# Layer 3 of a graph network: transposes on row halves, reciprocals by DMA, W_out product over two units

## The chip, the cores and the metric

The kernel runs on one core of a Trainium2 chip. The core has a matrix engine (TensorE, written PE in the profile; its weight loads are a row of their own, PEld), a vector engine (VectorE, DVE), a scalar engine (ScalarE, ACT), a general engine (GpSimd, POOL) and a queue engine (SyncE, SP), which here only starts DMAs. Each engine works through its own list of instructions in order; semaphores tie them together. PE writes to PSUM[...] and DVE or ACT take the results from there to SBUF. The metric is the time of one execution in microseconds (us), as the median of three runs.

## The reference

The input x holds 32 graphs of 512 nodes with 64 features. One adjacency matrix adj (512 x 512, scaled, mostly zero) serves all. There are four layers, each of the form x = x + f(relu(layernorm(x))). Layer 0 is a graph convolution, layer 1 two rounds of it, layer 2 an attention layer with additive scores. Most of the time goes to layer 3:

```python
def gat_layer(x, graph, W, b):
    h = x @ W
    s = jnp.einsum('bnd,bmd->bnm', h, h) * graph
    s = jnp.where(s == 0.0, NEG_INF, s)
    a = jax.nn.softmax(s, axis=2)
    return jnp.einsum('bnm,bmd->bnd', a, h) + b
heads = jax.vmap(lambda W, b: gat_layer(flow_x, graph, W, b))(Wh, bh)   # 8 heads, 128 wide
x = jax.nn.leaky_relu(cat, negative_slope=0.01)     # cat: the heads side by side, 1024 wide
out = gat_layer(x, graph, W_out, b_out)             # 64 wide
return jax.nn.leaky_relu(out, negative_slope=0.01)
```

So each graph needs nine 512 x 512 softmaxes in layer 3 and one in layer 2. Everything is 32-bit floating point.

## The kernel before

Layers 0 and 1 run first, to about 260 us. Layers 2 and 3 are one pipeline over *units*, built by `run` near the end of the kernel. A unit is two softmaxes of 512 x 512, called k = 0 and 1, and there are 160 of them: 16 `Gat` units (layer 2, two graphs each), 128 `Heads` units (layer 3, one graph and two heads each, so four per graph) and 16 `Out` units (the last attention of layer 3, two graphs each). An Out unit stands after the third Heads unit of the graph that follows its two graphs, so in the steady part eight Heads units and one Out unit make up one repeat. The last Out unit stands alone, after three empty places.

A unit is worked in four steps, one for each block of 128 rows, r = 0 to 3. Step number k of the loop in `run` issues, in this order, the work of several units:

- `scores` (L545 to L550) of the current unit: one product for each of the two softmaxes, into `s_ps`, which has two buffers of two PSUM banks.
- `transpose` of the unit that began five steps ago. For block j of columns it turns the exponentials `p_att` around, eight blocks of 128 x 128 on PE, into two PSUM tiles `pt_ps` (L413), and ACT copies each tile to `pt_att` (L418).
- `recips` of the same unit, when j is 1. DVE takes the reciprocals of the row sums (L432). These lie one per partition; the later multiplication needs them along the free dimension, the same in all 64 partitions of a half. Eight products with a broadcast reciprocal as the weights and the identity as the moving matrix do this (L436), and ACT copies the result to `recb` (L444).
- `values` of the block transposed one step before: two products into `av` (L425), which is summed over four steps.
- `end` of the unit that began ten steps ago. `end(0)` multiplies `av` by `recb` on DVE (`o_att`, L448); for Heads `end(1)` makes two products `y_ps` (L619) and ACT turns them into the heads' outputs `cat` (L624); for Out `end(2)` transposes back and adds to x (L454, L456), and SP stores the result (L675).
- `prep` of the next unit. For Heads, step 2 makes `g` (L591, L599), and the first unit of a graph makes the normalised input `hn` and its transpose `hx` in step 0. For Out, the steps 0 to 3 multiply `cat` by `W_out`, two of the eight heads in each, into one PSUM tile `gT_ps` (L642); step 3 then copies it to `gT` and transposes that to `gV` (L648 to L653).
- `soft` of the current unit: DVE multiplies the scores by adj (L536), finds zeros (L540) and, for each k, adds the mask and takes the row minimum of the negated scores (L397); ACT takes the exponential and the row sum (L401).

Eight PSUM banks are in use: four for the scores, one for `av`, and three in the pool `ps_m`, from which the tiles `pt_ps`, `rec_ps`, `y_ps`, `g_ps`, `gT_ps`, `hx_ps`, `gV_ps` and `back_ps` are all taken. `recb` has two buffers.

The kernel is written with the Tile layer, which puts in the semaphores. It also places each engine's instructions when the program is built, so an instruction can stand earlier or later on its engine than the order of the calls says. No planner of the kernel's own is involved, and the SP and POOL queues have nothing in this part but the output stores.

## Time and profile before

| | us |
|---|---|
| median of three runs (lowest, highest) | 2912.98 (2911.55, 2920.7) |
| the profiled execution, its own time | 2918.14 |
| span of that execution, first to last instruction | 2916.4 |
| PE busy | 2813.4 (96%) |
| PE weight loads busy | 1380.0 (47%) |
| DVE busy | 2407.5 (83%) |
| ACT busy | 2049.0 (70%) |
| POOL busy | 52.7 (2%) |

The profile is of one execution. A group of instructions is named by the line of the kernel, the engine, the operation, and what it writes and reads; its duration is the mean of one instruction, and "idle before" is the time for which the engine stood still just before it, with the instruction that released it. Matmuls overlap, so the duration of one matmul is more than its share of the engine's time; the distance from one start to the next is what a matmul costs. In a timeline each row is a start, a length, the engine, and how many like instructions were merged into the row; in brackets stands the idle time before it and what ended it.

### The profile page before, as it was taken

Reading aid. Unit: us, or ns where it says so; the run is one execution under the profiler, and the core shown is the slowest. Engines: PE = TensorE matmul, PEld = TensorE weight load, DVE = VectorE, ACT = ScalarE, POOL = GpSimd, SP = SyncE. Lnnn points to the kernel's source line nnn. Section 1 sums busy time; section 2 is a strip of 40 time slices with the busy share of each in tenths; the row PEclk is TensorE's granted clock in tenths of the full one; section 3 lists DMA queues with packets and bytes.
Section 4 is the critical chain, followed back from the end, with each engine's and each line's share of the span. In section 5 each row is a group of like instructions: output and inputs, shape, how many; then the busy total and the mean of one; then the engine's idle time right before and its main releaser. Section 6 shows DMA issues by size and latency. Waiting matters only on the chain.

```text
span 2916.4 us, 41809 instructions
## 1 busy us (share of the span) xinstructions
PE 2813.4 (96%) x15532; PEld 1380.0 (47%) x15532; DVE 2407.5 (83%) x4870; ACT 2049.0 (70%) x4687; POOL 52.7 (2%) x49
## 2 busy tenths in 40 slices
PE   7998887899999999999999999999999999999998
PEld 4555544444444444444444444444444444444443
DVE  6665889899798988888888888888888888888884
ACT  2333767677777778777777777777777777777775
POOL 3000000000000000000000000000000000000000
PEclk9998999899999999999999999999999999999999
DMA  3000000000000000000000000000000000000000
GB/s 86 1 1 1 1 1 1 1 1 1 1 5 4 1 4 1 4 1 5 1 4 1 4 1 4 1 5 1 4 1 5 1 5 1 4 1 4 1 4 4
DMA packets 9916, 13.10 MB, mean 4 GB/s; under 512 B 1016, under 2 KB 9376, under 8 KB 9584
## 3 DMA queue, kind: packets, MB, share of 16 engines
q1 hardware_dynamic: 4752, 5.24, 0.5%
q10 hardware_dynamic: 4208, 4.19, 0.5%
q8 instruction: 122, 2.00, 0.3%
q0 software_dynamic: 752, 0.99, 0.2%
q14 instruction: 82, 0.67, 0.1%
HBM read 6.23 MB, written 4.19 MB: 4 GB/s over the span
## 4 chain that ended last, share of the span: by engine, by line
PE 88%; DVE 6%; ACT 3%; issue 1%; POOL 1%; DMA 1%; POOLq 0%; DVEq 0%; ACTq 0%
PE av L425 20%; PE pt_ps L413 20%; PE s_ps L547 19%; PE rec_ps L436 6%; PE g_ps L591 5%; PE y_ps L619 4%; PE nt_ps L240 4%; PE gT_ps L642 3%; PE nt1b_ps L240 2%; ACT p_att L401 1%; DVE s_att L536 1%; PE po L251 1%; DVE t_att L397 1%; PE wh_ps L474 1%; DVE l_att L397 1%
## 5 line engine op out<-in xcount | busy, mean ns | idle before, releaser
L401 ACT ACTIVATE p_att<-t_att,negmax 128x512 f32<-128x512 f32 x1152 | 825.3, 717 | 466.3 <-DVE negmax L397 466.2
L536 DVE TENSOR_TENSOR s_att<-s_ps,adj_p 128x1024 f32<-128x1024 f32 x576 | 703.3, 1221 | 228.6 <-PE s_ps L547 228.6
L413 PEld LDWEIGHTS pt_ps<-ident,p_att 128*128 128x128 f32 x5120 | 554.8, 142 | 492.6 <-ACT p_att L401 187.5
L418 ACT COPY pt_att<-pt_ps 128x512 f32<-128x512 f32 x1280 | 679.3, 581 | 120.7 <-PE pt_ps L413 120.5
L397 DVE CUSTOM_DVE_ANT_0 t_att<-s_att,t_att 128x512 f32<-128x512 f32 x1152 | 752.3, 687 | 13.4
L413 PE MATMUL pt_ps<-ident,p_att 128*128 128x128 f32 x5120 | 714.5, 282 | 12.6 <-ACT p_att L401 7.5
L547 PE MATMUL s_ps<-hx,g 64*128 64x512 f32 x2048 | 661.2, 625 | 2.0 <-DVE s_att L536 2.0
L425 PE MATMUL av<-pt_att,hn 128*64 128x512 f32 x2048 | 579.0, 611 | 0.0
L540 DVE TENSOR_SCALAR t_att<-s_att 128x1024 f32<-128x1024 f32 x576 | 393.1, 683 | 24.3 <-ACT pt_att L418 0.5
L547 PEld LDWEIGHTS s_ps<-hx,g 64*128 64x128 f32 x2048 | 204.8, 185 | 311.3 <-issue 121.3
L401 ACT ACTIVATION_READ_ACCUMULATOR p_att<-t_att,negmax 128x1 f32 x1152 | 216.0, 187 | 0.0
L436 PE MATMUL rec_ps<-ident,rec 128*64 128x128 f32 x2560 | 186.6, 284 | 16.9 <-DVE rec L432 10.6
L436 PEld LDWEIGHTS rec_ps<-ident,rec 128*64 128x64 f32 x2560 | 144.4, 139 | 50.6 <-issue 26.5
L624 ACT ACTIVATE cat<-y_ps,bh 128x512 f32<-128x512 f32 x256 | 159.6, 672 | 4.4 <-PE y_ps L619 4.4
L425 PEld LDWEIGHTS av<-pt_att,hn 128*64 128x64 f32 x2048 | 115.6, 135 | 76.5 <-issue 76.2
L619 PE MATMUL y_ps<-o_att,wh_sb 64*128 64x512 f32 x512 | 145.8, 641 | 1.6 <-ACT pt_att L418 0.8
L591 PE MATMUL g_ps<-hx,m 64*128 64x512 f32 x256 | 144.6, 645 | 1.0 <-ACT pt_att L418 0.9
L642 PE MATMUL gT_ps<-cat,wo_sb 128*64 128x512 f32 x512 | 131.4, 595 | 0.0
L448 DVE TENSOR_TENSOR o_att<-av,recb 128x512 f32<-128x512 f32 x160 | 108.9, 681 | 21.8 <-PE av L425 20.6
L240 PE MATMUL nt_ps<-adj_t,hn 128*128 128x512 f32 x256 | 116.5, 598 | 0.0
L397 DVE DVE_READ_ACCUMULATOR2_ANT negmax<- 128x1 f32 x1280 | 104.7, 82 | 0.0
L444 ACT COPY recb<-rec_ps 128x512 f32<-128x512 f32 x160 | 93.9, 587 | 8.8 <-PE rec_ps L436 8.8
(131 smaller groups left out, 1930.4 us busy)
## 6 DMA issues: line engine op xcount, KB each, us to landing
out_dram<-x SPq DMA_DIRECT2D x32, 128.0 KB, 1.8
x<-in_x_dram ACTq DMA_DIRECT2D x3, 1024.0 KB, 13.7
x<-in_x_dram ACTq DMA_DIRECT2D x4, 256.0 KB, 7.9
adj_raw<-in_adj_dram SPq DMA_DIRECT2D x1, 1024.0 KB, 5.3
wh_sb<-in_L_gnn_Wh_dram POOLq DMA_DIRECT2D x2, 256.0 KB, 8.0
wo_sb<-in_L_gnn_W_out_dram POOLq DMA_DIRECT2D x1, 256.0 KB, 7.9
wl<-in_L_gnn_net_params_dram POOLq DMA_DIRECT2D x4, 16.0 KB, 7.0
bias_b<-in_L_gnn_bias_dram POOLq DMA_DIRECT2D x1, 32.0 KB, 7.6
```

The lines of the kernel that those rows point to most:

```text
L240: nc.tensor.matmul(p, lhsT=lhs(k), rhs=adj_t[:, k, :], start=(k == 0), stop=(k == C - 1))
L397: nc.vector.tensor_tensor_reduce(out=ns[k], in0=s[k], in1=t[k], scale=-1.0, scalar=BIG, op0=OP.add, op1=OP.min, accum_out=self.negmax[:, k ...
L401: nc.scalar.activation(self.p[:, k, r, :], ns[k], AF.Exp, bias=self.negmax[:, k, r : r + 1], scale=-1.0, accum_out=self.sum[:, k, r : r + 1],)
L413: nc.tensor.transpose(ps[:, r * P : (r + 1) * P], self.p[:, k, r, j * P : (j + 1) * P], ident,)
L418: nc.scalar.copy(pt[:, k, :], ps)
L425: nc.tensor.matmul(self.av[halves(k), :], lhsT=self.v(k, j), rhs=pt[:, k, :], start=(j == 0), stop=(j == C - 1),)
L436: nc.tensor.matmul(ps[halves(k), r * P : (r + 1) * P], lhsT=rec[:, k, r : r + 1].to_broadcast([P, F]), rhs=ident, start=True, stop=True,)
L536: nc.vector.tensor_tensor(s, ps, adj_f[:, r, None, :].to_broadcast([P, 2, N]), OP.mult)
L540: nc.vector.tensor_scalar(t, s, 0.0, FLOW_NEG, op0=OP.is_equal, op1=OP.mult)
L547: nc.tensor.matmul(u.s_ps[:, k], lhsT=g[halves(k), r * P : (r + 1) * P], rhs=x[halves(k), :], start=True, stop=True,)
L591: nc.tensor.matmul(ps, lhsT=m2[rows, 2 * i : 2 * i + 2, :].rearrange("p h f -> p (h f)"), rhs=self.x[rows, :], start=True, stop=True,)
L619: nc.tensor.matmul(ps, lhsT=wh_sb[halves(k), h, :], rhs=self.o[halves(k), :], start=True, stop=True,)
```

## The change

There are four edits, all in the pipeline of units.

1. In `transpose` each 128 x 128 block is transposed as two halves of 64 rows. The half of rows 0 to 63 goes to one PSUM tile, the half of rows 64 to 127 to another, in turn, so both tiles of a step are filled together; ACT copies each tile to every second run of 64 elements of `pt_att`.
2. In `recips` the eight products, their PSUM tile and ACT's copy are gone. The reciprocals go into the first eight columns of a 128 x 32 tile, of which there are two, zeroed once by POOL. DVE transposes this tile in blocks of 32 x 32. Four DMAs on SP write the blocks' first eight rows to a small buffer in DRAM, and two more read it back as rows of 512, each to all 64 partitions of a half of `recb`.
3. `recips` is called when j is 0, one step earlier, and at the end of the step, after `soft`.
4. The product with `W_out` starts two units before the Out unit. One head is done in each step from the unit's step -7 to -2 and in its steps 0 and 1; `gT` is copied in step 1, and `gV` is made in step 2.

```diff
@@ pools and constants
+    dram = ctx.enter_context(
+        tc.tile_pool(name="dram", bufs=3, space=bass.MemoryType.DRAM)
+    )
...
+    recs = [const.tile([P, 32], F32, name=f"rec{i}") for i in range(2)]
+    for rec in recs:
+        nc.gpsimd.memset(rec, 0.0)
@@ Pair.transpose
+            ps = [ps_m.tile([P, 2, C, F], F32, name="pt_ps", tag="m") for half in range(2)]
             for k in range(2):
-                ps = ps_m.tile([P, N], F32, name="pt_ps", tag="m")
                 for r in range(C):
-                    nc.tensor.transpose(
-                        ps[:, r * P : (r + 1) * P],
-                        self.p[:, k, r, j * P : (j + 1) * P],
-                        ident,
-                    )
-                nc.scalar.copy(pt[:, k, :], ps)
+                    for half in range(2):
+                        nc.tensor.transpose(
+                            ps[half][:, k, r],
+                            self.p[halves(half), k, r, j * P : (j + 1) * P],
+                            ident[halves(half), halves(half)],
+                        )
+            pth = pt.rearrange("p k (r half q) -> p k r half q", r=C, half=2)
+            for half in range(2):
+                nc.scalar.copy(pth[:, :, :, half, :], ps[half])
@@ Pair.recips
-            rec = tiny.tile([P, 2, C], F32, name="rec")
-            nc.vector.reciprocal(rec, self.sum)
-            ps = ps_m.tile([P, N], F32, name="rec_ps", tag="m")
-            for r in range(C):
-                for k in range(2):
-                    nc.tensor.matmul(
-                        ps[halves(k), r * P : (r + 1) * P],
-                        lhsT=rec[:, k, r : r + 1].to_broadcast([P, F]),
-                        rhs=ident,
-                        start=True,
-                        stop=True,
-                    )
+            rec = recs[0]
+            recs.append(recs.pop(0))
+            nc.vector.reciprocal(rec[:, : 2 * C], self.sum.rearrange("p k r -> p (k r)"))
+            rect = tiny.tile([P, 32], F32, name="rect")
+            nc.vector.transpose(rect, rec)
+            row = dram.tile([2 * C, P], F32, name="rec_row")
+            for q in range(P // 32):
+                nc.sync.dma_start(
+                    row[:, q * 32 : (q + 1) * 32], rect[q * 32 : q * 32 + 2 * C, :]
+                )
             self.recb = wk.tile([P, N], F32, name="recb")
-            nc.scalar.copy(self.recb, ps)
+            for k in range(2):
+                nc.sync.dma_start(
+                    self.recb[halves(k), :],
+                    row[k * C : (k + 1) * C]
+                    .rearrange("(o r) p -> o (r p)", o=1)
+                    .to_broadcast([F, N]),
+                )
@@ Out.prep
-            if step == 0:
+            if step == -2 * C + 1:
                 self.gps = ps_m.tile([P, N], F32, name="gT_ps", tag="m")
-            if step < 4:
-                for h in (2 * step, 2 * step + 1):
-                    for k in range(2):
-                        nc.tensor.matmul(
-                            self.gps[halves(k), :], lhsT=wo_sb[:, h, :],
-                            rhs=Heads.cat[b + k, h], start=(h == 0), stop=(h == H - 1),
-                        )
-            if step == 3:
-                self.gT = wk.tile([P, N], F32, name="gT")
-                nc.scalar.copy(self.gT, self.gps)
+            h = H - 2 + step if step >= 0 else 2 * C - 1 + step
+            if 0 <= h < (H if step >= 0 else H - 2):
+                for k in range(2):
+                    nc.tensor.matmul(
+                        self.gps[halves(k), :], lhsT=wo_sb[:, h, :],
+                        rhs=Heads.cat[b + k, h], start=(h == 0), stop=(h == H - 1),
+                    )
+                if h == H - 1:
+                    self.gT = wk.tile([P, N], F32, name="gT")
+                    nc.scalar.copy(self.gT, self.gps)
+            if step == 2:
                 ps = ps_m.tile([P, C, P], F32, name="gV_ps", tag="m")
@@ run
                 u.transpose(j)
-                if j == 1:
-                    u.recips()
...
-            u, j = at(k, -C)
-            if u:
-                u.prep(j)
+            for early in range(2, -1, -1):
+                u, j = at(k, -C * (early + 1))
+                if u and (early == 0 or isinstance(u, Out)):
+                    u.prep(j - early * C)
             if cur:
                 cur.soft(r)
+            u, j = at(k, C + LAG)
+            if u and j == 0:
+                u.recips()
```

## The prediction

> **What bounds the kernel now.** I read the page's busy shares first, then one repeat of layer 3, then engine timelines inside it. Layer 3 repeats: its nine units (eight Heads, one Out; 36 steps) begin their o_att multiplications 16.4, 22.04, 15.8, 15.0, 14.5, 15.1, 15.5, 15.0 and 14.9 us apart, 144.26 in sum, again and again from about 600 us to 2870 us: 2270 / 144.26 = 15.75 repeats. One of them, busy time by engine:

> ```profile
> 1000.00:1144.26 144.26, 144.03 (x818) 67.43 (x816) 123.32 (x244) 109.12 (x253) 0.00 (x0) 1.00 0.01 3
> ```

> The columns are PE, weight loads, VectorE (DVE), ScalarE (ACT), POOL, clock. PE is never idle: PE sets 144.26. DVE has 21 us to spare. The PE timeline of one step, in order:

> ```profile
> 1504.00 1.02 PE L547 MATMUL s_ps<-hx,g 64*128 64x512 f32 x4
> 1504.95 1.09 PE L413 MATMUL pt_ps<-ident,p_att 128*128 128x128 f32 x8
> 1505.98 1.08 PE L425 MATMUL av<-pt_att,gV 128*64 128x512 f32 x4
> 1506.99 1.13 PE L547 MATMUL s_ps<-hx,g 64*128 64x512 f32 x4
> ```

> Start to start: scores 0.95 to 1.06, transposes 1.03, values 1.01. The single transposes start 0.109 apart (8 x 0.109 = 0.87); the rest is the 0.09 after the last one.

> **The DVE step**, as it runs when nothing holds it:

> ```profile
> 1507.41 0.69 DVE L397 CUSTOM_DVE_ANT_0 t_att<-s_att,t_att 128x512 f32<-128x512 f32 x1
> ...
> 1508.65 1.22 DVE L536 TENSOR_TENSOR s_att<-s_ps,adj_p 128x1024 f32<-128x1024 f32 x1
> 1509.90 0.69 DVE L540 TENSOR_SCALAR t_att<-s_att 128x1024 f32<-128x1024 f32 x1
> 1510.51 0.68 DVE L448 TENSOR_TENSOR o_att<-av,recb 128x512 f32<-128x512 f32 x1
> 1511.11 0.68 DVE L397 CUSTOM_DVE_ANT_0 t_att<-s_att,t_att 128x512 f32<-128x512 f32 x1
> ```

> This step, with o_att, is 1511.11 - 1507.41 = 3.70; the next one, without it, 3.20 (3.21 from the unrounded starts). So a unit is 4 x 3.21 + 0.49 = 13.33 of DVE.

> **The wait that decides.** Once in nine units (at the Out unit) the reciprocal of the row sums already stands on DVE directly behind the last minimum of its unit. DVE, then ACT:

> ```profile
> 1469.52 0.68 DVE L397 CUSTOM_DVE_ANT_0 t_att<-s_att,t_att 128x512 f32<-128x512 f32 x1
> 1470.13 0.08 DVE L397 DVE_READ_ACCUMULATOR2_ANT negmax<- 128x1 f32 x1
> 1472.34 0.20 DVE L432 RECIPROCAL rec<-sum_att 128x8 f32<-128x8 f32 x1 [2.12 <-ACT p_att L401]
> ```

> ```profile
> 1469.64 0.72 ACT L401 ACTIVATE p_att<-t_att,negmax 128x512 f32<-128x512 f32 x1 [1.09 <-DVE negmax L397]
> ...
> 1470.36 1.25 ACT L624 ACTIVATE cat<-y_ps,bh 128x512 f32<-128x512 f32 x2
> 1471.50 0.71 ACT L401 ACTIVATE p_att<-t_att,negmax 128x512 f32<-128x512 f32 x1
> 1472.11 0.19 ACT L401 ACTIVATION_READ_ACCUMULATOR p_att<-t_att,negmax 128x1 f32 x1
> ```

> The sum needs the last exponential, which stands behind two cat activations: DVE idles 2.12. In the eight other units an s_att (1.25) stands before the reciprocal, which then waits 0.3 to 0.4. Under a PE bound this costs nothing.

> [...] the score matmuls of the two halves start 7 ns apart. [...] here 0.09 to 0.10 between scores and transposes, none from y to scores. [...]

> **The change, part by part.**

> 1. Half transposes. Each 128x128 transpose becomes two of 64 rows x 64 columns: 16 a step. The trace has that form eight times, at setup, in one row group:

> ```profile
> 262.45 0.57 PEld L354 LDWEIGHTS whT_ps<-ident,wh_sb 64*128 64x128 f32 x8 [1.05 <-PE po1b L251]
> 262.49 0.68 PE L354 MATMUL whT_ps<-ident,wh_sb 64*128 64x64 f32 x8 [0.89 <-PE po1b L251]
> ```

> Eight weight loads of 0.14 in 0.57: starts 0.062 apart, and so the matmuls'. Two row groups overlapped: 8 x 0.062 = 0.50 instead of 0.87; not overlapped: 16 x 0.062 = 0.99. I take 0.50 (16 reciprocal matmuls in two column groups ran 0.109 a pair), and keep both. [...] together -0.5 a step, -2.0 a unit.

> 2. Reciprocal matmuls leave PE: 16 passes in 0.82 a unit. ACT's recb copy (0.59) goes too; ACT isn't the bound. PE gains 2.8 a unit: 144.26 - 9 x 2.8 = 119.

> 3. In their place: a 128x32 DVE transpose, not in the trace, and six DMAs on SP. In 8 of 9 units the transpose stands between s_att and the t_att that depends on it, where the reciprocal stood before for nothing (1.14 + 0.12 against 1.25). So 0, at most 0.2 x 160 = 32 us. The DMAs: [...] the trace has 1.8 for the output stores. Estimate for writes, then reads: 5 us[...]. recb is needed five steps, some 18 us, later. Hidden; without that cover o_att would wait 5 us in each unit. SP is otherwise idle; its two output stores stand between rec_row writes and wait less than a step.

> 4. The reciprocal moves. The built program's order (no times are in it) puts it, in 8 of 9 units, directly behind the last minimum and ahead of the next s_att; in the ninth, whose last step has no cats, s_att comes first. ACT's order there stays exponential, cat, cat, exponential. From the start of the last minimum, S, to the reciprocal's is 1472.34 - 1469.52 = 2.81; the slot was free 0.61 after S, so 2.20 is lost, plus 0.12 for itself: 13.33 + 2.32 = 15.65 a unit. Everything on DVE stands behind it, first s_att, whose scores PE has long delivered; ACT then waits for minimums. DVE never catches up. A repeat: 8 x 15.65 + 13.33 = 138.5; hn3 and hx copies, about 1.3 for each of two images; back, 0.6. DVE with ACT: 141.7, above PE's 119. This takes the place of the PE bound.

> 5. The W_out product: 32 passes, 6.8 us, lay in 4 steps (the 22.04 interval); now one head (0.86) goes in each of eight steps. Its PSUM buffer, one of three in the pool, is held over nine steps instead of four, and a step's transposes now fill two. First held unit: in step 2 g fills one of the two left, and its copy on ACT stands behind that step's two exponentials, over 1.57 after the step's own S; the copy takes 0.47. Only then do step 3's transposes start: with 0.5 for them, 0.3 of latencies and two copies of 0.47 they are through at 3.8, which is S + 0.6 of step 3, where ACT would have been free at S + 0.12. First exponential to S + 1.35; y, in the same buffers, ready by 1.7; two cats to 2.85; second exponential and its sum to 3.67. The reciprocal starts at 3.68 instead of 2.81: +0.85. In the second held unit PE is the bound: scores 0.96, transposes 0.59, values 1.01, W_out 0.86 are 3.42 a step against 3.21, and g with the scores take 1.82 instead of 0.96. Followed step by step from that reciprocal, s_att waits 0.25, 0.25, 0 (that step has o_att) and 0.95: +1.45. Together 2.3: 144.0 a repeat, against 144.26.

> 6. Elsewhere: layer 2 is DVE-bound (16.04 a unit, reciprocal behind a whole step as before): -2. The tail, PE-bound from 2868 to 2886: shorter transposes, no reciprocal matmuls, part of the product in idle slots: -5. Two POOL memsets at the start: 0, POOL is idle.

> Sum: 15.75 x (144.0 - 144.26) = -4, -2, -5: -11. Against the profiled execution's own 2918.14 (span 2916.4) 2907; the median of the runs is 5 below that execution: **2902**. The copies' 64-element runs I take at the old 0.58; 0.1 more would add some 6 us by the held-buffer units.

> **Rivals.**

> - The held buffer costs nothing (PE's lead of some 2 us absorbs it): 141.7 a repeat, -40 - 7: 2866. For it: the lead. Against: PSUM is short by count.
> - The reciprocal's wait isn't exposed: DVE's own 124 plus 2.3, -18 x 15.75 - 7: about 2625. Against it: [...]the 2.12 stands in the trace.
> - Slower: the halves don't overlap. Outside the held units nothing changes (PE 14 against 15.65); inside, +0.5 over eight steps is +4 a repeat, +63: 2965. It decides from about 0.075 a pair of halves instead of 0.062: 0.013 x 8 pairs x 8 steps = 0.8 a repeat, the whole gain. For it: no such pair in the trace, and 32 instructions in 0.5 us is denser than its densest (32 in 0.82).
> - The clock: in layer 2, where PE idles, it was granted 0.77 to 0.94. At 0.9 PE's 119 is 132, still under 141.7; only the held units would feel it. It adds to the case above.
> - The DMA path is late and o_att waits: it would have to be over 18 us. 2950 or more.

> **How the numbers follow.** 0.3% is 9 us, about what a measurement can tell. Forecast case 0.45, its own range 2885 to 2925; free buffer 0.20; unexposed 0.07; no overlap 0.25; late DMA 0.03. Faster (under 2904): half of the forecast case, 0.23, + 0.20 + 0.07 = 0.50. Same: 0.17. Slower: 0.25 + 0.03 + 0.05 = 0.33. The range 2845 to 2968 leaves out the unexposed case and the far ends of the others, about 0.17.

> **What would show it.** Per repeat: PE busy down to some 120, DVE idle up; the reciprocal's idle time on DVE from 70.8 us in all to about 2.2 x 125 = 270, released by p_att; no rec_ps; pt_ps starts in pairs, eight pairs in 0.5; recb landing long before o_att; unit intervals near 15.6 instead of 15.0, and no 22. Wrong if the reciprocal waits under 1 us, if pairs start 0.1 apart, or if o_att is released by a DMA.

## The result: 0.7% slower, where 0.4% faster was forecast

| | before | after |
|---|---|---|
| median of four runs each (lowest, highest), us | 2914.91 (2911.55, 2920.7) | 2937.81 (2932.46, 2939.57) |
| ratio, 95% interval | | 1.0073 [1.0052, 1.0095] |
| profiled execution, own time / span, us | 2918.14 / 2916.4 | 2932.46 / 2930.7 |

The time lies in the range that was given, 2845 to 2968, but on the wrong side of the kernel before: some 21 us slower by the ratio (23 between the medians) instead of 11 us faster. In the profiled executions the difference is 14.3 us. The profiled execution of the changed kernel is the shortest of its four; where the other three spend 5 us more isn't in a trace.

**The profile after.** The page's busy line, its engines on the chain that ended last, and two of its groups (busy us, mean ns, then idle time before and its releaser):

```profile
PE 2565.6 (88%) x18092; PEld 1169.9 (40%) x18092; DVE 2404.9 (82%) x5030; ACT 1969.1 (67%) x4527; POOL 52.9 (2%) x51
...
DVE 60%; PE 21%; ACT 12%; issue 5%; POOL 1%; DMA 0%; POOLq 0%; DVEq 0%; ACTq 0%
...
L446 DVE RECIPROCAL rec<-sum_att 128x8 f32<-128x8 f32 x160 | 32.2, 201 | 290.5 <-ACT p_att L408 290.5
...
L465 DVE TENSOR_TENSOR o_att<-av,recb 128x512 f32<-128x512 f32 x160 | 108.7, 679 | 23.5 <-PE av L436 23.5
```

PE lost 248 us of work and is no longer what sets the pace: 60% of the chain is DVE. The reciprocal now waits 290.5 us for the last exponential (70.8 before, about 270 forecast). `o_att`, the user of the DMA path, waits for PE alone and never for a DMA.

One repeat of layer 3 of the changed kernel, from `o_att` to `o_att` nine units later (columns as in the window of the kernel before: PE, weight loads, DVE, ACT, POOL, clock; behind it the DMA engines' busy share and GB/s):

```profile
1040.63:1184.82 144.19, 128.44 (x962) 54.66 (x960) 123.03 (x254) 104.65 (x244) 0.00 (x0) 1.00 0.06 20
```

PE fell from 144.03 to 128.44 of it, and yet the repeat is 144.19 instead of 144.26. (PE was forecast at some 120. Where the other 8 us are is left open; either figure is below the repeat.) The DVE and ACT timelines of the changed kernel at the end of an ordinary unit show why:

```profile
1353.78 0.69 DVE L404 CUSTOM_DVE_ANT_0 t_att<-s_att,t_att 128x512 f32<-128x512 f32 x1
1354.40 0.08 DVE L404 DVE_READ_ACCUMULATOR2_ANT negmax<- 128x1 f32 x1
1356.60 0.20 DVE L446 RECIPROCAL rec<-sum_att 128x8 f32<-128x8 f32 x1 [2.12 <-ACT p_att L408]
1356.71 1.17 DVE L553 TENSOR_TENSOR s_att<-s_ps,adj_p 128x1024 f32<-128x1024 f32 x1
1357.80 0.20 DVE L448 STREAM_TRANSPOSE rect<-rec 128x32 f32<-128x32 f32 x1
1357.93 0.69 DVE L557 TENSOR_SCALAR t_att<-s_att 128x1024 f32<-128x1024 f32 x1
```

```profile
1353.90 0.72 ACT L408 ACTIVATE p_att<-t_att,negmax 128x512 f32<-128x512 f32 x1 [0.81 <-DVE negmax L404]
...
1354.62 1.25 ACT L641 ACTIVATE cat<-y_ps,bh 128x512 f32<-128x512 f32 x2
1355.76 0.71 ACT L408 ACTIVATE p_att<-t_att,negmax 128x512 f32<-128x512 f32 x1
1356.37 0.19 ACT L408 ACTIVATION_READ_ACCUMULATOR p_att<-t_att,negmax 128x1 f32 x1
```

It is the wait of the kernel before, to 0.01 us, but now in nearly every unit and with DVE as the bound: ordinary units are 15.67 us long (forecast 15.65). The 32x32 transpose lies between `s_att` and the `t_att` that needs it, for nothing, as forecast.

**Where the 14.3 us are.** From the starts of the 160 `o_att` in both traces (us):

| stretch | before | after | difference | forecast |
|---|---|---|---|---|
| start to the first `o_att` | 315.6 | 316.6 | +1.0 | 0 |
| layer 2, first to 16th | 276.2 | 281.9 | +5.6 | -2 |
| first repeat | 144.6 | 152.9 | +8.3 | -0.3 |
| next 14 repeats | 2019.8 | 2023.3 | +3.5 | -3.6 |
| last nine units | 154.1 | 149.5 | -4.6 | -5 |
| after the last `o_att` | 6.0 | 6.5 | +0.5 | 0 |

So the length of a steady repeat was foreseen, and the sign was lost in layer 2, in the first repeat and in a part of the later ones.

### The profile page after: what moved, and what is told of

The parts are those of the page before. It is cut to its first block, busy times and chain, and to the rows that moved or that the text cites. A ratio compares the mean times of both kernels' runs of the same rounds, so it can differ in the third digit from the quotient of the medians.

```text
span 2930.7 us, 48553 instructions
## 1 busy us (share of the span) xinstructions
PE 2565.6 (88%) x18092; PEld 1169.9 (40%) x18092; DVE 2404.9 (82%) x5030; ACT 1969.1 (67%) x4527; POOL 52.9 (2%) x51
## 4 chain that ended last, share of the span: by engine, by line
DVE 60%; PE 21%; ACT 12%; issue 5%; POOL 1%; DMA 0%; POOLq 0%; DVEq 0%; ACTq 0%
DVE s_att L553 20%; DVE t_att L404 19%; DVE t_att L557 9%; ACT p_att L408 7%; ACT cat L641 4%; PE nt_ps L240 4%; PE av L436 4%; DVE o_att L465 3%; PE pt_ps L422 3%; PE nt1b_ps L240 2%; PE s_ps L564 2%; PE y_ps L636 2%; DVE l_att L524 1%; PE gT_ps L661 1%; DVE l_att L404 1%
## 5 line engine op out<-in xcount | busy, mean ns | idle before, releaser
L564 PE MATMUL s_ps<-hx,g 64*128 64x512 f32 x2048 | 746.4, 635 | 3.0 <-DVE s_att L553 3.0
L422 PE MATMUL pt_ps<-ident,p_att 64*128 64x64 f32 x10240 | 557.3, 232 | 199.8 <-ACT cat L641 72.7
L422 PEld LDWEIGHTS pt_ps<-ident,p_att 64*128 64x128 f32 x10240 | 462.3, 142 | 636.2 <-ACT pt_att L429 262.8
L553 DVE TENSOR_TENSOR s_att<-s_ps,adj_p 128x1024 f32<-128x1024 f32 x576 | 697.4, 1211 | 13.7 <-PE s_ps L564 12.1
L436 PE MATMUL av<-pt_att,hn 128*64 128x512 f32 x2048 | 554.7, 619 | 39.3 <-DVE o_att L465 39.3
L564 PEld LDWEIGHTS s_ps<-hx,g 64*128 64x128 f32 x2048 | 233.0, 187 | 309.5 <-issue 123.0
L446 DVE RECIPROCAL rec<-sum_att 128x8 f32<-128x8 f32 x160 | 32.2, 201 | 290.5 <-ACT p_att L408 290.5
L636 PE MATMUL y_ps<-o_att,wh_sb 64*128 64x512 f32 x512 | 255.4, 664 | 8.4 <-ACT pt_att L429 8.4
L636 PEld LDWEIGHTS y_ps<-o_att,wh_sb 64*128 64x128 f32 x512 | 73.7, 190 | 185.0 <-ACT pt_att L429 106.2
L436 PEld LDWEIGHTS av<-pt_att,hn 128*64 128x64 f32 x2048 | 103.8, 135 | 78.4 <-issue 46.3
L240 PE MATMUL nt_ps<-adj_t,hn 128*128 128x512 f32 x256 | 117.1, 601 | 0.0
L408 ACT ACTIVATE p_att<-l_att,negmax 128x512 f32<-128x512 f32 x128 | 91.8, 721 | 34.2 <-DVE negmax L404 33.5
```

The costliest lines, as they stand in the source:

```text
L240: nc.tensor.matmul(p, lhsT=lhs(k), rhs=adj_t[:, k, :], start=(k == 0), stop=(k == C - 1))
L408: nc.scalar.activation(self.p[:, k, r, :], ns[k], AF.Exp, bias=self.negmax[:, k, r : r + 1], scale=-1.0, accum_out=self.sum[:, k, r : r + 1],)
L422: nc.tensor.transpose(ps[half][:, k, r], self.p[halves(half), k, r, j * P : (j + 1) * P], ident[halves(half), halves(half)],)
L436: nc.tensor.matmul(self.av[halves(k), :], lhsT=self.v(k, j), rhs=pt[:, k, :], start=(j == 0), stop=(j == C - 1),)
L553: nc.vector.tensor_tensor(s, ps, adj_f[:, r, None, :].to_broadcast([P, 2, N]), OP.mult)
L564: nc.tensor.matmul(u.s_ps[:, k], lhsT=g[halves(k), r * P : (r + 1) * P], rhs=x[halves(k), :], start=True, stop=True,)
```

## The experiments

"The changed kernel" is the one of the diff above; of an edit that takes over one of its parts only the main lines are shown. Times are medians, and a ratio is to the kernel before, measured on the same chip beside it.

### Each part alone, and the reciprocal put back in its place

The builder of the program decides where an instruction stands on its engine. `tc.keep_in_program_order` holds one where the order of the calls puts it. In the first run the reciprocal is held behind the minimums of the step in which it is called, two steps after the last exponential of its unit:

```diff
-            nc.vector.reciprocal(rec[:, : 2 * C], self.sum.rearrange("p k r -> p (k r)"))
+            tc.keep_in_program_order(
+                nc.vector.reciprocal(rec[:, : 2 * C], self.sum.rearrange("p k r -> p (k r)"))
+            )
```

> The changed kernel with one difference: the reciprocal is pinned on VectorE behind the work traced before it, so that it stands two whole steps after the last minimum of its unit. Theory (the reciprocal's wait for the exponentials, 2.12 us in 8 of 9 units, sets the time): the idle time before the reciprocal falls from 290 us to under 20, a unit's interval from 15.67 to about 13.5, a repeat from 144.2 to about 128; time about 2665, between 2640 and 2720. Rival (PSUM shortage and the lower TensorE clock set it, the wait only hides them): within 15 us of the changed kernel.

The second, third and fourth take one part of the change each and leave the rest as before: edit 1 (half transposes), edits 2 and 3 (reciprocals by DMA, called behind the step), edit 4 (W_out product over two units).

```diff
@@ e2: Pair.transpose of the changed kernel, all else as before
-                ps = ps_m.tile([P, N], F32, name="pt_ps", tag="m")
+            ps = [ps_m.tile([P, 2, C, F], F32, name="pt_ps", tag="m") for half in range(2)]
...
@@ e3: Pair.recips of the changed kernel and its call behind soft(), all else as before
-            ps = ps_m.tile([P, N], F32, name="rec_ps", tag="m")
...
+            row = dram.tile([2 * C, P], F32, name="rec_row")
...
@@ e4: Out.prep of the changed kernel and its calls, all else as before
-            if step == 0:
+            if step == -2 * C + 1:
                 self.gps = ps_m.tile([P, N], F32, name="gT_ps", tag="m")
...
```

> The kernel before with the half transposes alone. In the built program the reciprocal stands in front of s_att in 124 units already. Theory (this place costs 2.1 us a unit and takes back what TensorE gains): a unit about 15.6, the W_out burst still adds 2 to 4 us to its unit, time 2910 to 2950, although TensorE's work falls by 2.0 us a unit. Rival (the loss comes from the DMA path or the spread product): TensorE stays the bound and 2.0 us x 144 units are gained: about 2630.

> The kernel before with the reciprocals by DMA alone; the reciprocal stands behind s_att in 124 units, as in the kernel before. Theory: TensorE stays the bound and loses 0.82 us a unit: 2795, between 2780 and 2820; recb lands long before o_att. Rival (the DMA path costs time): 2913 or more.

> The kernel before with the W_out product over two units alone. Theory: TensorE is the bound and its work is the same, so 2900 to 2925; the 22.04 us interval disappears and others grow. Rival (holding one of three PSUM buffers over nine steps stalls TensorE by itself): 2930 to 2960.

| | median us | ratio, 95% interval |
|---|---|---|
| e1, reciprocal held | 2805.75 | 0.9612 [0.9596, 0.9628] |
| e2, half transposes alone | 3004.18 | 1.0294 [1.0278, 1.0309] |
| e3, reciprocals by DMA alone | 2838.07 | 0.9722 [0.9704, 0.974] |
| e4, W_out product spread alone | 2923.1 | 1.0011 [1.0003, 1.0019] |

The place of one 0.2 us instruction is worth 132 us. Spreading the product alone (e4) changes 0.1%, as its theory had it. Alone, the half transposes, which take PE work away, make the kernel slower by 2.9%. The page of e2 says why, in the reciprocal's group:

```profile
L436 DVE RECIPROCAL rec<-sum_att 128x8 f32<-128x8 f32 x160 | 32.2, 201 | 266.3 <-ACT p_att L401 266.3
```

With the half transposes the builder puts the reciprocal directly behind the last minimum, as in the changed kernel; with the DMA part alone (e3) it stands behind the next `s_att` in most units and waits 111.5 us in all. So it is the half transposes, not the call's new place, that move the reciprocal, and the DMA part, which touches the reciprocal, is the one that gains. Both kernels are slower than their ranges, e2 by 54 us and e3 by 18: ordinary units of e2 are 16.05 us long and not 15.6, and `s_att` waits another 117.1 us there for scores; those of e3 lost 0.55 us and not 0.82 (e12 below shows most of the reason).

e1 went the way of the theory, but by half of what it expected (2665). Its groups of `s_att` and the third DVE pass, on the page:

```profile
L555 DVE TENSOR_TENSOR s_att<-s_ps,adj_p 128x1024 f32<-128x1024 f32 x576 | 697.6, 1211 | 130.9 <-PE s_ps L566 124.6
...
L559 DVE TENSOR_SCALAR t_att<-s_att 128x1024 f32<-128x1024 f32 x576 | 398.5, 692 | 46.9 <-ACT pt_att L429 1.8
```

In the changed kernel these two waited 13.7 and 24.0 us. Of the 287 us that the reciprocal no longer waits, 140 came back there. Ordinary units are 14.09 us, not the 13.5 assumed, and the two units of a repeat in which the W_out tile holds one of the three buffers are 17.38 and at least 17.26. The PE and DVE timelines of e1 in the first of them:

```profile
1400.81 0.71 PE L422 MATMUL pt_ps<-ident,p_att 64*128 64x64 f32 x15 [1.21 <-ACT g L618]
1401.45 1.08 PE L436 MATMUL av<-pt_att,hn 128*64 128x512 f32 x4
1402.46 1.35 PE L638 MATMUL y_ps<-o_att,wh_sb 64*128 64x512 f32 x4
1403.74 1.08 PE L663 MATMUL gT_ps<-cat,wo_sb 128*64 128x512 f32 x4
1404.75 1.13 PE L566 MATMUL s_ps<-hx,g 64*128 64x512 f32 x4
```

```profile
1402.92 0.08 DVE L404 DVE_READ_ACCUMULATOR2_ANT negmax<- 128x1 f32 x1
1405.92 1.23 DVE L555 TENSOR_TENSOR s_att<-s_ps,adj_p 128x1024 f32<-128x1024 f32 x1 [2.92 <-PE s_ps L566]
```

The transposes wait until ACT's copy of `g` has read its buffer, and everything behind them on PE is late, the next scores too: DVE stands still for 2.92. Whether the half transposes must fill two buffers at once wasn't shown: no run here tried one for both halves.

### The held buffer, the half transposes with the reciprocal held, and layer 2

```diff
@@ e6: e1 with Out.prep and its calls of the kernel before; e8: the changed kernel with the same
-            if step == -2 * C + 1:
+            if step == 0:
                 self.gps = ps_m.tile([P, N], F32, name="gT_ps", tag="m")
...
@@ e7: e2 with recips called when j is 0, behind soft(), and
-            nc.vector.reciprocal(rec, self.sum)
+            tc.keep_in_program_order(nc.vector.reciprocal(rec, self.sum))
```

> The changed kernel with the reciprocal held in its place (as in the earlier run) and the W_out product back in four steps of one unit. Theory: with the reciprocal out of the way, the two units in which the W_out tile holds a buffer of the pool are what is left (17.4 and 17.3 to 18.8 us instead of 14.1; DVE waits 131 us for scores in all), some 8 us a repeat; the burst costs about 5 in its place. A repeat goes from 136.5 to about 133, the total to about 2750 (2725 to 2780). Rival: the held tile is no cause, the spread takes a PE burst away and undoing it costs 3 to 6 a repeat: 2850 or more; if both cancel, 2795 to 2815.

> The changed kernel with the W_out product back in four steps of one unit, nothing else. Theory: with DVE and ACT as the bound, spreading the product is worth the burst of some 4 to 5 us less the held tile's 2.3 us a repeat: without it a repeat takes 145 to 147, the total 2950 to 2985. Rival: the held tile costs more than the burst: 2925 or less.

> Half transposes alone (reciprocals by products on PE, old W_out product), but the reciprocal called behind the step's work and held there. Theory: half transposes alone took 3004 only because the reciprocal moved in front of the scores and waited 17 us a repeat; held in its place the ordinary units fall from 16.05 to about 14.2 and the repeat from 149.5 to 133 (130 to 136): 2750 (2720 to 2790). Rival: the half transposes themselves cost time (two tiles filled at once, copies in runs of 64 elements): still 2900 or more.

A clean repeat is one that has the full clock throughout.

| | median us | ratio, 95% interval | clean repeat, us |
|---|---|---|---|
| the changed kernel | 2937.81 | 1.0073 [1.0052, 1.0095] | 144.19 |
| e8, its W_out product in four steps | 2950.63 | 1.0118 [1.0101, 1.0135] | 145.62 |
| e1, reciprocal held | 2805.75 | 0.9612 [0.9596, 0.9628] | 135.84 |
| e6, e1 with the product in four steps | 2821.74 | 0.9671 [0.9655, 0.9687] | 137.04 |
| e7, half transposes, products on PE, held | 3039.81 | 1.0421 [1.0405, 1.0437] | 151.08 |

e8 is at the low end of its theory: spreading the product is worth 1.4 us a repeat. It also gives the held buffer its price: the two units of 16.97 and 17.40 us are 15.67 and 16.29 in e8, so it costs 2.4, and the product in four steps 3.85 (19.52 instead of 15.67). e6 missed. With the reciprocal held, the buffer costs 4.0 in a clean repeat (17.38 and 17.26 against 14.09 and 16.52), not the 8 that I had read from the idle time, and the product in four steps 5.2 (19.59 against 14.36): undoing the spread loses 1.2.

e7 missed by 290 us, and in its direction. The reciprocal no longer waits (3.1 us in all), but the kernel is slower than with the wait. Its DVE and PE timelines:

```profile
1481.71 0.20 DVE L436 RECIPROCAL rec<-sum_att 128x8 f32<-128x8 f32 x1
1481.82 1.17 DVE L540 TENSOR_TENSOR s_att<-s_ps,adj_p 128x1024 f32<-128x1024 f32 x1
...
1486.65 1.22 DVE L540 TENSOR_TENSOR s_att<-s_ps,adj_p 128x1024 f32<-128x1024 f32 x1 [1.58 <-PE s_ps L551]
```

```profile
1481.96 1.09 PE L440 MATMUL rec_ps<-ident,rec 128*64 128x128 f32 x16 [0.20 <-DVE rec L436]
1482.98 0.71 PE L415 MATMUL pt_ps<-ident,p_att 64*128 64x64 f32 x16
```

The products with the reciprocal stand on PE in front of the step's transposes, its values and the next scores. PE can start them only when the reciprocal is there, at 1481.96, and then has 4.6 us of work before DVE's next scores, against a DVE step of 3.2: DVE waits 1.58 (375 us for scores in the whole run). The wait did not go; it moved from DVE to PE and back. With the reciprocals by DMA nothing on PE waits for them: holding the reciprocal took 129 us away there (e8 to e6), where it added 36 here (e2 to e7, which differ in the place of the call too). So the DMA part is worth more than the PE time that it removes; how much of the 36 comes from the moved call isn't shown.

### Layer 2: the clock

Layer 2 was forecast 2 us shorter and became 5.6 us longer. Windows of both kernels over the start and the length of layer 2 (columns as above); the kernel before, then the changed one:

```profile
265.00:316.00 51.00, 41.61 (x194) 29.02 (x196) 38.26 (x96) 28.33 (x64) 0.00 (x0) 0.67 0.00 0
316.00:395.00 79.00, 64.56 (x390) 38.05 (x389) 71.55 (x159) 54.63 (x124) 4.57 (x2) 0.91 0.00 1
395.00:475.00 80.00, 65.46 (x390) 38.56 (x387) 71.15 (x158) 55.87 (x127) 4.57 (x2) 0.89 0.00 1
475.00:600.00 125.00, 107.03 (x614) 58.08 (x613) 112.54 (x249) 87.74 (x201) 4.57 (x2) 0.92 0.00 1
```

```profile
265.00:316.00 51.00, 40.03 (x224) 27.15 (x224) 37.83 (x95) 26.59 (x61) 0.00 (x0) 0.63 0.02 6
316.00:395.00 79.00, 59.70 (x435) 34.05 (x434) 69.41 (x159) 49.46 (x113) 4.57 (x2) 0.79 0.05 15
395.00:475.00 80.00, 62.32 (x432) 35.90 (x430) 67.34 (x151) 49.44 (x115) 4.57 (x2) 0.71 0.05 14
475.00:600.00 125.00, 100.04 (x728) 52.88 (x728) 112.23 (x258) 86.45 (x198) 4.56 (x2) 0.80 0.05 16
```

```diff
@@ class Gat (layer 2), which had no scores()
+        def scores(self, r):
+            ps = ps_s.tile([P, 2, N], F32, name="fill_ps", tag="s_ps")
+            for k in range(2):
+                nc.tensor.matmul(
+                    ps[:, k], lhsT=ident[halves(k), :], rhs=adj_f[halves(k), r, :],
+                    start=True, stop=True,
+                )
```

> The changed kernel, with two more products per step in the 16 units of layer 2 whose result nobody uses (extra work on PE, of the size of layer 3's score products; outputs are the same). Theory of the clock: PE stood still so often in layer 2 that the granted clock fell to 0.71 to 0.80 there, and that is why the 16th o_att came at 598.4 instead of 591.8 us. With the products PE is busy, the clock goes above 0.93 between 316 and 600 us, the 16th o_att comes at 590 to 594, and the whole takes 5 to 9 us less than the changed kernel: 2925 to 2934. Rival: the clock isn't the cause, the six DMAs and the new order on DVE are; then the extra products change nothing or make it slower: 2937 to 2950, 16th o_att at 598 or later.

> As the first run with extra products in layer 2 (changed kernel, result unused), but of 256 columns instead of 512. With 512 the built program also ordered layer 2's work on DVE and ACT differently; with 256 the order is the changed kernel's but for a few neighbours that swap places, so this run separates the clock from the order. Theory of the clock: the granted clock between 316 and 600 us rises from 0.71-0.80 to 0.85-0.95, the 16th o_att comes at 588 to 594 instead of 598.4 us, and the whole takes 2926 to 2933. Rival, the new order alone gave the 20 us: the time stays at 2935 to 2942 and the 16th o_att at 597 or later.

> The kernel before with the same extra products of 512 columns in layer 2 (result unused). If they help by the clock that the change lowers in layer 2 (0.88 to 0.94 before, 0.71 to 0.80 after), the kernel before gains less than the changed one did (20): 3 to 12 us, 2905 to 2916. If they help by the order in which the program was built, the kernel before gains as much, 15 to 22: 2896 to 2903.

> The kernel before with the extra products of 256 columns in layer 2 (result unused). It tells whether the 22 us that they gave the changed kernel undo a loss that the change brought in, or are a gain open to any version. Theory: the change brought in the low clock; the kernel before, granted 0.88 to 0.94 there, gains under 8 us: 2910 to 2920, 16th o_att at 586 or later. Rival: most of the gain comes from the start of layer 2, where the kernel before also had a low clock (0.67 between 265 and 316 us): it gains 10 to 16: 2901 to 2908, 16th o_att at 576 to 582; then the change's own loss in layer 2 is only the rest.

> The changed kernel with the reciprocal held behind the step's work and with the extra products of 512 columns in layer 2 (result unused). The two gains lie in different stretches of time and should add: 2805.75 less about 20: 2785 (2778 to 2794). Rival: with the reciprocal held, layer 2's order is another and the products collide with it: 2800 or more.

> The changed kernel with the reciprocal held behind the step's work and with the extra products of 256 columns in layer 2 (result unused). The changed kernel gained as much from 256 columns as from 512, so here too: 2785 to 2790; its order in layer 2 is that of the kernel with the reciprocal held, so a gain says again that the clock is the cause. Rival, order: 2800 or more.

| | columns | median us | ratio, 95% interval | 16th `o_att` at, us |
|---|---|---|---|---|
| the changed kernel | none | 2937.81 | 1.0073 [1.0052, 1.0095] | 598.4 |
| e5 | 512 | 2917.74 | 1.0001 [0.9993, 1.001] | 577.1 |
| e9 | 256 | 2915.37 | 0.9994 [0.9985, 1.0003] | 580.3 |
| the kernel before | none | | 1 | 591.8 |
| e10 | 512 | 2916.19 | 0.9994 [0.9986, 1.0003] | 587.3 |
| e13 | 256 | 2923.11 | 1.0035 [1.0021, 1.0049] | 596.6 |
| e1 | none | 2805.75 | 0.9612 [0.9596, 0.9628] | 598.8 |
| e11 | 512 | 2788.03 | 0.9568 [0.9551, 0.9586] | 581.0 |
| e14 | 256 | 2783.04 | 0.9562 [0.9548, 0.9576] | 575.1 |

The windows of e9 over the same stretches:

```profile
265.00:316.00 51.00, 46.99 (x344) 28.78 (x343) 45.14 (x113) 33.92 (x79) 0.00 (x0) 0.90 0.04 12
316.00:395.00 79.00, 69.93 (x574) 44.21 (x573) 73.19 (x167) 52.63 (x121) 4.57 (x2) 0.94 0.05 15
395.00:475.00 80.00, 66.07 (x521) 40.17 (x520) 71.40 (x164) 53.48 (x122) 4.57 (x2) 0.88 0.05 15
475.00:600.00 125.00, 99.10 (x736) 49.87 (x736) 112.91 (x246) 82.63 (x191) 6.42 (x3) 0.83 0.06 18
```

Products that nobody reads make the changed kernel 22 us faster and bring it level with the kernel before; in the traces 18.1 us of it are gained by the 16th `o_att`. A matmul of `e_ps` takes 822 ns in e9, one of `wh_ps` 341. ACT's wait for `pt_ps` and DVE's for `e_ps`, 38.3 and 14.6 us before and 47.9 and 18.8 after (between 300 and 600 us), are 37.5 and 8.4 in e9. The order of DVE and ACT in e9 is that of the changed kernel but for neighbours that swap places, so the order isn't the cause; e14 repeats this on e1, whose 16th `o_att` comes 23.7 us earlier. In e5 and e11 the order is another, and the gain is about the same. The expectations of e5 and e9 named too small a gain: half of it comes before the first `o_att`, in the start of layer 2 (307.9 instead of 316.6), where the clock was low in both kernels (0.67 and 0.63) and where they had counted none. From the first to the 16th `o_att` e9 takes 272.3 us, 3.9 less than the kernel before: with the clock up, layer 2 gains, as the forecast had it.

The kernel before gained nothing from such products, and both runs are slower than expected, e10 by 0.2 us and e13 by 3. It too reaches its first `o_att` 7 to 8 us earlier, but layer 2 then takes 2.8 and 12.6 us more. Why isn't shown: PE is busy 76 of 80 us there in e13, but e10, with more extra work, loses less, and in both the order of DVE and ACT in layer 2 is far from that of the kernel before. Nor is the clock all that counts: e7, granted 0.86 to 0.91, takes 285.7 us for layer 2, more than the changed kernel.

The low clock comes with the half transposes and the DMA part together. The four kernels that have both and no extra products (the changed one, e1, e6, e8) spend 36 to 40 stretches of 3.413 us at half clock between 316 and 600 us; the six others without extra products spend 15 to 20. PE in e2 is busy no longer (60.7 of 80 us between 395 and 475) than in the changed kernel (62.3, at a lower clock), and yet its clock is 0.89.

What stood ahead of the changes can be counted. Take PE's busy share in each stretch of 3.413 us and the clock of the next one, in the traces of the kernel before and the changed one from 260 us on. At full clock, the half clock followed on 20 of 24 stretches in which PE was busy less than 50%, and on 2 of 1404 with 65% or more. At half clock, the full one followed on none of 23 stretches with less than 65%, on 2 of 13 with 65 to 95%, and on 28 of 50 with 99.5% or more. So in these two traces the clock went with PE's pauses within one such stretch. Between 316 and 600 us it went down 12 times in the changed kernel and 7 times in the kernel before.

### A wait under PE as the bound

```diff
@@ e12: e3 with the reciprocal held as in e1
-            nc.vector.reciprocal(rec[:, : 2 * C], self.sum.rearrange("p k r -> p (k r)"))
+            tc.keep_in_program_order(
+                nc.vector.reciprocal(rec[:, : 2 * C], self.sum.rearrange("p k r -> p (k r)"))
+            )
```

> Reciprocals by DMA alone, with full transposes and the old W_out product, and the reciprocal held behind the step's work. In the run of the DMA part alone the reciprocal waited 112 us in all, but PE was busy 99% in layer 3. Theory: under PE as the bound the wait costs nothing, so taking it away changes nothing: 2838 within 6, repeat still 139.2 us. Rival: the wait costs DVE time in any case: 2800 or less, or, if holding the reciprocal itself hurts (a worse place in layer 2), 2845 or more.

Measured: 2822.03, ratio 0.9679 [0.9665, 0.9693], 16 us less than e3. A repeat went from 139.16 to 138.24, so the theory that the wait is free under a busy PE fell too. The PE timelines of the step with `cat`, e3 and then e12:

```profile
1407.85 1.42 PE L420 MATMUL pt_ps<-ident,p_att 128*128 128x128 f32 x8
1409.21 1.08 PE L432 MATMUL av<-pt_att,hn 128*64 128x512 f32 x4
```

```profile
1401.56 1.18 PE L420 MATMUL pt_ps<-ident,p_att 128*128 128x128 f32 x8
1402.67 1.08 PE L432 MATMUL av<-pt_att,hn 128*64 128x512 f32 x4
```

Eight transposes take 1.02 elsewhere, 1.36 here in e3 and 1.11 in e12. PE stood between the fourth and the fifth: they start 0.386 and 0.144 apart instead of 0.109, because the fifth needs the buffer of a `y_ps` that ACT's `cat` still reads (both are of the same pool). The row of merged instructions counts that as busy (PE is busy 495 and 497 of 500 us). A busy share of 99% still held 0.25 us a unit that ACT decided.

## Why the prediction was wrong

Three terms of its sum were off: layer 2, taken as bound by DVE; the first repeat, counted like the others; and the held buffer, to which the clock adds in five repeats. Steps 1 to 4 held.

**Step 1, half transposes: right.** The PE timeline of the changed kernel:

```profile
1342.28 0.66 PE L422 MATMUL pt_ps<-ident,p_att 64*128 64x64 f32 x16
1342.87 1.08 PE L436 MATMUL av<-pt_att,hn 128*64 128x512 f32 x4
```

From the first of sixteen half transposes to the first product behind them it is 0.59 (1.02 before, with eight whole ones); pairs start 0.061 to 0.063 apart (0.062 taken), so the two halves run together and the rival that they don't is out. From the last pair of scores to the first transposes it is 0.42 (0.52 before). Both make 0.53 a step, where 0.5 was counted. ACT's copies in runs of 64 elements take 0.58, as before.

**Step 2, reciprocal products: right as work.** 0.82 us a unit was counted. Where PE is the bound and only this changes, ordinary units lost 0.80 with the reciprocal held (14.96 to 14.16, e12) and 0.55 without (14.41, e3): the rest is the wait for a buffer just shown. It is not what the changed kernel is bound by.

**Step 3, the DMA path: right.** The queue of SP for the unit above, whose `rect` was written by 1358.00:

```profile
1358.03 1.29 SPq L451 DMA_DIRECT2D rec_row<-rect  x4
1360.28 1.09 SPq L456 DMA_DIRECT2D recb<-rec_row  x2
```

The last packets of `recb` move at about 1363.2, 5.2 us after `rect` (5 estimated). It is hidden.

**Step 4, the reciprocal's wait: right.** 15.67 against 15.65 a unit, 2.12 each; e1 shows that it is worth 132 us, and e2 that the half transposes bring it in.

**Step 5, the held buffer: right in a clean repeat, mis-sized over all.** It costs 1.3 in the first unit and 1.1 in the second, 2.4 in all (0.85, 1.45 and 2.3 worked out), and without it a repeat would be 144.19 - 2.42 = 141.8 (141.7 worked out). But five of the 14 repeats are 0.9 to 1.4 longer, 5.5 us in all, nearly all of it in the second held unit. Windows over that unit, in six repeats of the changed kernel; the clock is the third column from the end:

```profile
878.12:896.44 18.32, 16.70 (x118) 7.78 (x114) 14.13 (x31) 11.63 (x27) 0.00 (x0) 0.91 0.01 3
1023.23:1040.63 17.40, 15.51 (x118) 6.94 (x114) 14.14 (x31) 11.64 (x27) 0.00 (x0) 1.00 0.03 10
1167.42:1184.82 17.40, 15.50 (x118) 6.94 (x114) 14.14 (x32) 11.65 (x27) 0.00 (x0) 1.00 0.01 4
1311.89:1330.41 18.52, 16.90 (x118) 7.07 (x114) 14.14 (x31) 11.64 (x27) 0.00 (x0) 0.91 0.01 2
1457.18:1474.59 17.41, 15.52 (x118) 6.94 (x114) 14.15 (x32) 11.64 (x27) 0.00 (x0) 1.00 0.01 4
1745.57:1764.27 18.70, 16.99 (x118) 6.86 (x114) 14.14 (x31) 11.64 (x27) 0.00 (x0) 0.91 0.01 3
```

0.91 over 18.3 us is 0.09 x 18.3 / 0.5 = 3.3 us at half clock; in the trace it is one stretch of 3.41. In this trace, e5 and e9 together, this unit of the 14 repeats is longer than 17.41 whenever the clock is 0.91, and never at 1.00. PE stands still ahead of it, once in the first held unit and once in the second (timeline of PE, the repeat of the last window):

```profile
1735.18 0.71 PE L422 MATMUL pt_ps<-ident,p_att 64*128 64x64 f32 x15 [1.23 <-ACT g L616]
...
1753.02 0.71 PE L422 MATMUL pt_ps<-ident,p_att 64*128 64x64 f32 x15 [1.62 <-ACT g L616]
```

The transposes wait for ACT's copy of `g` in both. The prediction had this wait in the first unit alone and took PE for the bound in the second, so that the sum of 2.3 came out is in part luck. The pause of 1.62 us goes with the half clock. The trace of the changed kernel has it 14 times in layer 3: six times it lies within one of the stretches of 3.413 us, and the next stretch has the half clock each time; eight times two stretches share it, and the next has the full clock each time. None of the 15 pauses of 1.23 us is followed by the half clock. In the same 14 repeats of the kernel before, PE pauses for less than 0.3 us at a time and the half clock doesn't come. The prediction named the clock and said that only the held units would feel it, but gave it no time.

**The count of 15.75 repeats: failed.** All repeats were taken alike, but the first has no W_out burst that could be saved, and the units pay all the same: nine intervals went from 144.6 to 152.9, +8.3 (149.8 in e8, without the held buffer). At the other end no buffer is held in the first six of the last nine intervals, and these saved 4.5 of the 4.6. That equals the forecast of the last stretch, but not for its reason: the last three intervals, with the PE-bound tail, stayed as they were (56.6 after, 56.7 before), where 5 us were to be saved.

**Step 6, layer 2: failed, and with it the sign.** "DVE-bound: -2" took layer 2 for a place where PE's speed doesn't count. From its first to its 16th `o_att` DVE was busy 247.6 of 276.2 us before, 246.9 of 281.9 after and 246.7 of 272.3 in e9: its work is the same, and its waits differ. DVE and ACT wait there for products of PE, the change takes PE work away and the clock with it, and +5.6 came out, besides +1.0 before its first `o_att`. e9 puts it the other way round: with the clock up, the changed kernel has the time of the kernel before, and layer 2 is 3.9 us shorter than in it.

The sum over the steps: +7.6 in layer 2, +8.6 in the first repeat, +7.1 in the next 14 and +2 elsewhere lie between the forecast of -11 and the +14.3 of the trace.

**The rivals.** A free buffer (2866) is out by e8, which has 15.67 and 16.29 us where the held units have 16.97 and 17.40. An unexposed wait (2625) is out by the 290.5 us; even where the wait is gone, in e1, the time is 2806, since the price of the held buffer and waits for scores stand behind it. A late DMA is out by `o_att`. The rival on the slow side had the wrong mechanism; the remark on the clock was the right one and had no chance of its own.

## What to carry to other kernels

Where a builder orders the queues, changing some instructions can move another: look for what now stands in front of the long operation, and hold the one that waits for a far result behind work that doesn't (here 132 us for a 0.2 us instruction). When the bound leaves TensorE, price the clock too, in each stage apart (here it went from about 0.9 to between 0.71 and 0.80 in layer 2), those first where other engines wait for its products while TensorE has pauses of its own; work that is of no use can pay there (here 22 us, though nothing in the kernel before). Holding an instruction paid here only where nothing on PE waited for what is held: with half transposes, the reciprocals had to leave PE first.

## What was not expected of the hardware

- Two products a step whose result nobody reads made the changed kernel 0.8% faster (2937.81 to 2915.37), with the order of DVE and ACT all but unchanged and the granted clock up from 0.79 to 0.94 and from 0.71 to 0.88 in two windows of layer 2.
- The mean busy share of PE didn't tell the clock here: at 60.7 of 80 us busy it was 0.89 in e2, at 62.3 of 80 it was 0.71 in the changed kernel. In layer 3 of the changed kernel a pause of 1.62 us within one stretch of 3.413 us was followed by the half clock in 6 of 6 cases, one that two stretches shared in none of 8.
- The changed kernel with the reciprocal held and the extra products of 256 columns (e14) takes 2783.04, 0.9562 [0.9548, 0.9576] of the kernel before, the best of all that ran.
